# Replacing a list scheduler by written-out tables of order, engines, places and zero products in a two-layer transformer kernel

## The chip, the cores and the metric

The kernel runs on one core of one Trainium2 chip. The metric is the device time of one execution in microseconds (us). Engines are named as in the profile: PE is the matrix engine (TensorE), PEld its weight load, DVE is VectorE, ACT is ScalarE, POOL is GpSimd, and SP is SyncE, which here does nothing but issue DMAs. Each engine takes its instructions in the order in which the program lists them for it, and an instruction whose inputs are not ready holds up everything behind it on its engine.

## What is computed

The reference applies four residual blocks, each on a layer-normed input, to `x` of shape 8 x 512 x 128 in fp32:

```python
x = x + linear_attn(layernorm(x))     # 16 heads x 64; elu+1 features, q*KV/(q*Ksum+eps), wo, gelu
x = x + fp4_ffn(layernorm(x))         # both operands of each product rounded to blockwise FP4
x = x + causal_attn(layernorm(x))     # 16 heads x 8, softmax under a causal mask
x = x + routed_ffn(layernorm(x))      # rms norm, top 2 of 8 experts, low-rank (LoRA) experts on shared weights
```

The loop over the batch index b (0 to 7) is outermost; nothing of one b enters another b, so stages of different b can be run side by side.

## The kernel before, in words

`block_kernel` does not issue its instructions as it walks through the computation. Every call on `nc.tensor`, `nc.vector`, `nc.scalar`, `nc.gpsimd`, `nc.sync` or `nc.either` is recorded by `Plan.add` as a `Step`: one instruction, or several of one engine inside `one_go()`. There are 5166 steps. `nc.either` (the elementwise products of two SBUF tensors) leaves open whether DVE or POOL does the step. Only at the end does `plan.issue()` (line 1517) put all steps in an order, choose a buffer for each tile, and emit them; that is why nearly every row of the profile has one line, L407.

The stages are, for each b: `norm` (layer norm and transposition by `normed_T`, line 963), `linear` (`linear_attention`, line 978: for each of eight chunks of 128 features three 128x512 products on PE, elu on ACT and DVE, and for each pair of chunks in `products`, line 1015, one reciprocal of z0*z1 in two halves on DVE and five `either` products), `out` (`linear_out`, eight 128x512 products, gelu), `fp4` (`quantised`, line 1054: a chain of block maxima, scaling and rounding on DVE and `either`, followed by products), `attention` (`group`, line 1286: four groups of four heads; for each query tile the products of the next group's row maxima in `largest`, the products of this group in `scores`, the exponent on ACT, the causal cut on POOL, the product with v into `mid`), `routing`, and `experts` (line 1428: 34 products of 128x512 on PE for each b, a tanh on ACT, two multiply-adds on DVE and one `either` product for each of eight tiles). PSUM holds two tiles `pair` (two banks each), one `mid` and three `ahead`; an `ahead` tile can also be lent half a `pair`.

The order comes from `Plan.ordered` (line 249), a list scheduler: it walks along a planned time, and whenever an engine is free gives it the ready step of lowest rank. Ranks come from the table `TURNS` (line 706), which gives each stage of each b a span of due times. Durations come from the functions `cost` and `work`. The engines are asked in the order tensor, gpsimd, vector, scalar, sync, so that a ready `either` step is offered to POOL first. `Together` adds a dependence, that a group of products starts only when the inputs of all of them are ready. `Free` hands out the buffers. Last, `kept_warm` (line 365) puts products with zeros into planned gaps of PE (`plan.warmer`, line 907: a 128-row product of `ident` with zeros that is added to `mid`): they change no data and keep PE busy. 44 of them are issued, between 64 and 512 columns wide.

Of the kernel before, what the change touches and what calls it, by code (L numbers as in the profile page):

```python
# [17 lines left out]
P = 128  # L18
# [93 lines left out]
class Buf:  # L112


    def __init__(self, tag=None, place=None):
        self.tag, self.place = tag, place
        self.writer, self.readers = None, []
        self.first, self.users = None, {}


class Step:


    def __init__(self, number, engine, lane):
        self.number, self.engine, self.rank, self.lane = number, engine, 0.0, lane
        self.calls, self.needs, self.takes, self.uses = [], {}, [], {}
        self.cost, self.slow, self.port, self.size = 0.0, 0.0, False, 0
        self.work = 0.0
        self.start = self.end = None


TWO_PORTS = ("tensor_tensor", "scalar_tensor_tensor", "tensor_scalar", "tensor_copy")


class Plan:
# [3 lines left out]
    HOP = {"tensor": 0.1, "gpsimd": 0.1, "vector": 0.1, "scalar": 0.1, "sync": 0.2}  # L139

    def __init__(self, nc):
        self.nc, self.steps, self.open = nc, [], None
        self.lane, self.tags, self.psum, self.warmer = None, {}, (), None
        self.parts = {}
        self.engines = {n: Engine(self, n) for n in (*self.HOP, "either")}


    def tag(self, name, places, parts=None):

        self.tags[name] = list(places)  # L150
        self.parts[name] = parts or [((name, i),) for i in range(len(places))]
# [24 lines left out]

    def fixed(self, place):
        return View(Buf(place=place), place.shape)

# [4 lines left out]
    def together(self):  # L184
        return Together(self)

    def span(self, lane, low, high):
        return Span(self, lane, low, high)

    def add(self, engine, method, a, k):  # L190
        step = self.open
        if step is None:
            step = Step(len(self.steps), engine, self.lane)
            self.steps.append(step)
        elif step.engine is None:
            step.engine = engine
        assert step.engine == engine
        out = [k["out"]] if "out" in k else [a[0]]
        ins = [x for x in (*a[0 if "out" in k else 1 :], *k.values()) if isinstance(x, View)]
        if k.get("accum_out") is not None:  # L200
            out.append(k["accum_out"])
        step.calls.append((method, a, k))
        fast = "vector" if engine == "either" else engine
        if method is not None:
            step.cost += cost(fast, method, out[0], ins, a, k)
        if engine == "tensor" and method is not None:
            step.work += work(method, ins, a, k)
        if engine == "sync":
            step.size += 4 * out[0].shape[0] * _free(out[0])
        if engine == "either":  # L210
            step.slow += cost("gpsimd", method, out[0], ins, a, k)

        if engine == "gpsimd" and method != "memset":
            step.port = True
        elif engine in ("vector", "either") and method in TWO_PORTS:
            two = sum(v.shape[-1:] != (1,) or len(v.shape) > 2 for v in ins) > 1
            step.port |= (two or _free(out[0]) > 16) and not any(
                v.buf.tag in self.psum for v in (*ins, out[0]) if isinstance(v, View)
            )
        for v in ins:  # L220
            if all(v is not o for o in out) and isinstance(v, View):
                self.reads(step, v.buf)
        for v in out:
            if isinstance(v, View):
                self.writes(step, v.buf)

    def reads(self, step, buf):
        assert buf.writer is not None or buf.tag is None
        if buf.writer is not None and buf.writer is not step:
            step.needs[buf.writer] = True  # L230
        buf.readers.append(step)
        self.used(step, buf)

    def writes(self, step, buf):
        for s in (buf.writer, *buf.readers):
            if s is not None and s is not step:
                step.needs[s] = True
        buf.writer, buf.readers = step, []
        if buf.first is None and buf.tag is not None:
            buf.first = step  # L240
            step.takes.append(buf)
        self.used(step, buf)

    def used(self, step, buf):
        buf.users[step] = True
        step.uses[buf] = True


    def ordered(self):

        free = Free(self.parts)
        slots = {}
        left = {s: len(s.needs) for s in self.steps}
        then = {s: [] for s in self.steps}
        for s in self.steps:
            for n in s.needs:
                then[n].append(s)
        users = {}  # L260
        for s in self.steps:
            for b in s.uses:
                users[b] = len(b.users)
        ready_at = {s: 0.0 for s in self.steps}
        empties = set()
        for s in self.steps:
            for b in s.uses:
                if b.tag in self.psum and s.engine != "tensor" and (False or max(b.users, key=lambda u: u.number) is s):
                    empties.add(s)
        waiting = {e: [] for e in self.engines}  # L270
        for s in self.steps:
            if not left[s]:
                waiting[s.engine].append(s)
        turns = {}
        for s in sorted(self.steps, key=lambda s: (s.rank, s.number), reverse=True):
            for b in s.takes:
                turns.setdefault((s.lane, b.tag), []).append(b)
        busy = dict.fromkeys(self.engines, 0.0)
        port = 0.0
        moved = 0.0  # L280
        ends = []
        now, done, order, stuck = 0.0, 0, [], False
        clock = Clock()
        while done < len(self.steps):
            for e in self.HOP:
                while busy[e] <= now:
                    best, kept = None, set()
                    shared = waiting["either"] if e in ("vector", "gpsimd") else []
                    ready = [s for s in (*waiting[e], *shared) if ready_at[s] <= now]
                    ahead = HURRY if e == "tensor" and clock.idle(now) else 0.0  # L290
                    for s in sorted(
                        ready,
                        key=lambda s: (s.rank - (ahead if s.work > 0.6 * s.cost else 0.0) - (EMPTY if s in empties else 0.0), s.number),
                    ):
                        if s.port and port > now:
                            continue
                        asked = {}
                        for b in s.takes:
                            asked.setdefault(b.tag, []).append(b)
                        if not all(  # L300
                            all(b in turns[s.lane, t][-len(bs) :] for b in bs)
                            for t, bs in asked.items()
                        ):
                            continue
                        if all(
                            (t not in kept or stuck) and free.has(t, len(bs)) for t, bs in asked.items()
                        ):
                            best = s
                            break

                        kept.update(asked)
                    if best is None:
                        break
                    if any(
                        now < ready_at[s] <= now + PATIENCE and s.rank < min(best.rank - MARGIN, LIMIT)
                        for s in (*waiting[e], *shared)
                    ):
                        break
                    s, stuck = best, False
                    waiting[s.engine].remove(s)  # L320
                    if s.engine == "either":
                        s.engine = e
                        s.cost = s.slow if e == "gpsimd" else s.cost
                    for b in s.takes:
                        slots[b] = free.take(b.tag)
                        turns[s.lane, b.tag].remove(b)
# [6 lines left out]
                    if s.port:  # L333
                        port = busy[e]
# [1247 lines left out]
```

## Time and profile before

| | us |
|---|---|
| median of 3 runs | 1126.88 (1125.94 to 1127.14) |
| span of the profiled execution, first to last instruction | 1130.1 |
| PE busy in that span | 1040.2 (92%) |
| DVE busy | 830.3 (73%) |
| ACT busy | 630.8 (56%) |
| POOL busy | 624.3 (55%) |
| DMA engines, mean rate | 39 GB/s, of that 235 GB/s in the first 28 us |

No time but the span is given for the profiled execution itself; the span is 0.3% above the median of the three runs. In the profile's busy times the end of a product is modelled and lies behind the start of the next one, so that PE can be shown as fully busy while its products come at different distances. A product of fp32 operands stands as two rows in the profile. Of the DVE, successive instructions overlap by some 85 ns in the trace.

### The profile page before, as it was taken

The page shows a single profiled execution, that of the slowest core. Times are in us where ns is not written, and L with a number is a line of the kernel's source. Part 1 is how long each engine was busy: PE and PEld are TensorE (multiplying, and loading weights), DVE is VectorE, ACT ScalarE, POOL GpSimd, SP SyncE. Part 2 cuts the span into 40 slices and gives each one's busy share as a digit, 9 for nine tenths or more (in the row PEclk, how much of TensorE's full clock was granted, in tenths as well). Part 3 has the DMA queues.
Part 4 walks back from the last instruction along what each step waited for, and adds up shares of the span by engine and source line. Part 5 has one row for each costly group of instructions (what it writes and reads, how often), then busy time and mean ns, then how long its engine had stood idle before and what let it go on. Part 6 is the DMA issues. An engine that isn't in the chain of part 4 may idle for free.

```text
span 1130.1 us, 15043 instructions
## 1 busy us (share of the span) xinstructions
PE 1040.2 (92%) x5025; PEld 488.0 (43%) x5025; DVE 830.3 (73%) x1868; ACT 630.8 (56%) x1084; POOL 624.3 (55%) x669
## 2 busy tenths in 40 slices
PE   6667788998899999999998999999999999999998
PEld 2223333344344444444543444454454445445454
DVE  6868879897888967758788968788667765556543
ACT  5756787678786644644578555764443443344311
POOL 6647846676676466237635755467644533441534
PEclk9879989999999999999999999999999999999999
DMA  8000030001101020111012000210002102001000
GB/s 235 1 1 0 1 111 1 21 20 56 39 20 30 10 94 20 58 72 35 26 39 94 19 21 20 95 30 19 20 7 98 39 20 104 21 20 30 1 10 9
DMA packets 30572, 44.31 MB, mean 39 GB/s; under 512 B 4192, under 2 KB 18464, under 8 KB 30496
## 3 DMA queue, kind: packets, MB, share of 16 engines
q1 hardware_dynamic: 30496, 43.37, 11.9%
q8 instruction: 39, 0.64, 0.2%
q14 instruction: 37, 0.30, 0.1%
HBM read 23.95 MB, written 18.87 MB: 38 GB/s over the span
## 4 chain that ended last, share of the span: by engine, by line
PE 57%; DVE 15%; ACT 6%; issue 2%; POOL 1%; DMA 0%; POOLq 0%; DVEq 0%; ACTq 0%
PE ahead L407 31%; PE pair L407 19%; PE mid L407 7%; ACT pr L407 2%; DVE r L407 2%; DVE mx L407 2%; DVE h L407 1%; DVE sc L407 1%; ACT qf L407 1%; DVE s4 routing L407 1%; DVE qf L407 1%; DVE act L407 1%; ACT z L407 1%; DVE kf L407 1%; DVE oh L407 1%
## 5 line engine op out<-in xcount | busy, mean ns | idle before, releaser
L407 ACT ACTIVATE pr<-pair 128x1024 f32<-128x1024 f32 (+1 forms) x192 | 166.7, 879 | 149.2 <-PE pair L407 129.1
L407 DVE TENSOR_REDUCE mx<-pair 128x4 f32<-128x512 f32 (+2 forms) x192 | 198.5, 1041 | 68.4 <-PE pair L407 57.7
L407 POOL TENSOR_SCALAR_AFFINE_SELECT pr<-pr 128x256 f32<-128x256 f32 (+1 forms) x192 | 92.8, 485 | 176.4 <-ACT pr L407 175.6
L407 PE MATMUL pair<-qkT 32*128 32x128 f32 (+7 forms) x1024 | 172.3, 387 | 9.4 <-ACT pr L407 2.7
L407 PEld LDWEIGHTS pair<-qkT 32*128 32x128 f32 (+1 forms) x1024 | 84.4, 183 | 181.8 <-ACT pr L407 52.0
L407 POOL TENSOR_TENSOR act<-act,tw 128x512 f32<-128x512 f32 x64 | 81.3, 1272 | 88.8 <-DVE act L407 80.6
L407 PE MATMUL ahead<-um,b_sb 128*128 128x512 f32 x240 | 122.2, 607 | 0.0
L407 DVE RECIPROCAL r<-r 128x256 f32<-128x256 f32 x64 | 110.3, 1736 | 14.9 <-POOL r L407 14.8
L407 DVE SCALAR_TENSOR_TENSOR act<-act,ahead 128x512 f32<-128x512 f32 x120 | 81.9, 684 | 51.4 <-ACT act L407 38.0
L407 POOL TENSOR_TENSOR qa<-qa,qa 128x704 f32<-128x704 f32 (+4 forms) x60 | 81.2, 1354 | 35.1 <-DVE qa L407 26.2
L407 POOL TENSOR_TENSOR qf<-qf,r 128x512 f32<-128x512 f32 x64 | 80.5, 1278 | 34.5 <-DVE r L407 27.8
L407 PE MATMUL mid<-pr,va 128*10 128x512 f32 (+3 forms) x1024 | 93.3, 435 | 0.0
L407 POOL TENSOR_TENSOR qf<-qf,z 128x512 f32<-128x512 f32 x64 | 80.3, 1270 | 0.0
L407 ACT ACTIVATE act<-ahead 128x512 f32<-128x512 f32 x60 | 35.8, 597 | 72.0 <-PE ahead L407 71.9
L407 PE MATMUL ahead<-act,a_sb 128*128 128x512 f32 x128 | 65.2, 619 | 0.0
L407 POOL TENSOR_TENSOR r<-z,z 128x512 f32<-128x512 f32 x32 | 40.9, 1278 | 41.6 <-ACT z L407 39.3
L407 PE MATMUL ahead<-tT,w_sb 128*128 128x512 f32 x120 | 63.3, 609 | 0.0
L407 ACT ACTIVATE ahead<-ahead,bqkv_sb 128x512 f32<-128x512 f32 x96 | 63.0, 656 | 0.0
L407 PE MATMUL pair<-mask_q,ident 128*128 128x128 bf16 (+1 forms) x384 | 61.6, 242 | 0.0
L407 PE MATMUL ahead<-xnT,wk 128*128 128x512 f32 x100 | 56.7, 650 | 4.8 <-DVE kf L407 2.1
L407 PEld LDWEIGHTS ahead<-um,b_sb 128*128 128x128 f32 x240 | 40.7, 190 | 36.1 <-issue 29.6
L407 ACT ACTIVATE z<-qf,eps_sb,s 128x512 f32<-128x512 f32 x64 | 51.9, 811 | 6.8 <-DVE s L407 5.1
(227 smaller groups left out, 1986.4 us busy)
## 6 DMA issues: line engine op xcount, KB each, us to landing
stacks<-qk SPq DMA_DIRECT2D x32, 512.0 KB
qkT<-stacks SPq DMA_DIRECT2D x128, 128.0 KB
x<-in SPq DMA_DIRECT2D x8, 256.0 KB
qkT<-mr SPq DMA_DIRECT2D x128, 4.0 KB
out<-x SPq DMA_DIRECT2D x8, 256.0 KB
w_sb<-in SPq DMA_DIRECT2D x3, 256.0 KB
wq<-in SPq DMA_DIRECT2D x4, 128.0 KB
wk<-in SPq DMA_DIRECT2D x4, 128.0 KB
```

Of the source, the lines that this page charges most:

```text
L407: getattr(e, method)(*a, **k)
```

## The change

The scheduler goes: `Plan.ordered`, `kept_warm`, `Free`, `Together`, `Span`, `Clock`, `cost`, `work`, `TURNS` and every dependence that `Plan.add` kept for them. `Plan.issue` is given four tables instead: `ORDER`, the 5166 step numbers in the order in which they are issued; `ENGINES`, one letter for each `either` step; `PLACES`, one buffer number for each tile; and `ZEROS`, ten places in the order at which a product with zeros of a given width is put. Waits between engines are still set from the data that each instruction touches.

```diff
-    def issue(self):
-        for s in self.ordered():
-            for b in s.takes:
-                b.place = self.tags[b.tag][self.slots[b]]
+    def issue(self, order, engines, places, zeros):
+        engine = iter(engines)
+        for s in self.steps:
+            if s.engine == "either":
+                s.engine = {"v": "vector", "g": "gpsimd"}[next(engine)]
+        numbers = [
+            SIGNS.index(order[i]) * len(SIGNS) + SIGNS.index(order[i + 1])
+            for i in range(0, len(order), 2)
+        ]
+        assert sorted(numbers) == list(range(len(self.steps)))
+        place = iter(places)
+        for at, n in enumerate(numbers):
+            s = self.steps[n]
+            for b in s.takes:
+                b.place = self.tags[b.tag][int(next(place), 36)]
+            if at in zeros:
+                self.warmer(zeros[at])
             e = getattr(self.nc, s.engine)
...
+ORDER = (
+    "&3!!&1!H!K!I!)!J!L!O!N!M!P!Q!R!&!-$a$b!=!$$H$I$J!#$K$L$M!%$T$U$N!(!8&`&c$O!4$V$W!9!*$P!,"
...
+ENGINES = (
+    "vggggvggggvggggvgggggvvvgvggggggggvgggggvvggggvgggvggvggggggvggvgvgvgggggggggggggvvggggv"
...
+ZEROS = {
+    48: 512, 50: 384, 142: 512, 249: 256, 365: 192, 428: 512, 484: 512, 488: 320, 736: 512,
+    751: 256,
 }
...
     with tc.manual_schedule():
-        plan.issue()
+        plan.issue(ORDER, ENGINES, PLACES, ZEROS)
```

The recorded steps, their shapes and their number are the same in both kernels. Set side by side by engine, the two programs differ in this: 148 of the `either` steps that POOL does before are done by DVE after; 44 products with zeros become 10; and the order on every engine, SP's DMAs among them, is another.

## The prediction

> **What bounds the kernel now.** I first read the busy times of the page and then the same cut into four stretches. The cuts are not at equal times but at equal PE work. To get that work I took, for each kind of PE step, the start-to-start distance to the next step in the trace, and of each kind the lower quartile (the distance when nothing is late). These add up to 910 us for all steps but the products with zeros. The cuts stand where 150, 250 and 700 us of this work have been started.
>
> ```profile
> PE 1040.2 (92%) x5025; PEld 488.0 (43%) x5025; DVE 830.3 (73%) x1868; ACT 630.8 (56%) x1084; POOL 624.3 (55%) x669
> ```
> ```profile
> 0.00:247.20 247.20, 195.56 (x636) 84.08 (x637) 197.07 (x481) 170.82 (x300) 157.46 (x178) 0.93 0.15 45
> 247.20:372.80 125.60, 113.50 (x571) 52.99 (x570) 106.70 (x254) 95.97 (x174) 85.00 (x84) 1.00 0.10 35
> 372.80:884.70 511.90, 496.05 (x2614) 236.92 (x2613) 390.30 (x850) 280.55 (x477) 285.07 (x300) 1.00 0.13 43
> 884.70:1130.10 245.40, 235.14 (x1211) 113.99 (x1209) 136.25 (x285) 83.43 (x134) 96.74 (x108) 0.99 0.09 27
> ```
>
> The columns of the second view are the stretch, its length, busy PE, PEld, DVE, ACT, POOL, and PE's granted clock. A PE that is 92% busy looks as if nothing could be won. The timeline of PE in a dense place shows why that is misleading:
>
> ```profile
> 1091.71 1.02 PE L407 MATMUL ahead<-tT,w_sb 128*128 128x512 f32 x2
> 1092.57 1.02 PE L407 MATMUL ahead<-um,b_sb 128*128 128x512 f32 x2
> 1093.42 1.02 PE L407 MATMUL ahead<-tT,w_sb 128*128 128x512 f32 x2
> ```
>
> Each product is shown as 1.02 us long, but the next starts 0.86 us later. Counted so, the stretches lose 247 - 150 = 97 us, 126 - 100 = 26, 512 - 450 = 62 and 242 - 210 = 32 (its last product starts at 1126), 217 us together. Of this some 35 us have to be paid in any order: a 128-row product followed by one of the narrow attention products (32 rows, or 10 columns) starts the next one 95 ns later or more; there are 269 such changes before and 227 after, worth 26 and 22 us, and the head up to the first real product takes some 10.
>
> In the first stretch nothing is full: PE does 150 us of work in 247, and DVE, the busiest, stands at 80%. What it loses is waiting in a circle. The longest piece:
>
> ```profile
> 52.00:56.00 4.00, 0.00 (x0) 0.00 (x0) 3.30 (x13) 2.24 (x4) 2.51 (x3) 0.89 0.00 0
> 56.00:60.00 4.00, 0.00 (x0) 0.00 (x0) 2.73 (x2) 0.00 (x0) 3.68 (x3) 0.50 0.00 0
> ```
> ```profile
> 61.29 1.63 PE L407 MATMUL ahead<-ident,xn 128*128 128x128 f32 x4 [9.29 <-ACT xn L407]
> ```
>
> PE stands still for 9.3 us until the norm of b = 1 arrives, and the granted clock falls to 0.50.
>
> **The change, part by part.** *Engines.* 148 elementwise products go from POOL to DVE, 116 of 512 columns, 22 of 704 and 10 smaller.
>
> ```profile
> L407 POOL TENSOR_TENSOR act<-act,tw 128x512 f32<-128x512 f32 x64 | 81.3, 1272 | 88.8 <-DVE act L407 80.6 <-DVE s4 attention L407 5.2 <-DVE s4 routing L407 2.0
> L407 DVE SCALAR_TENSOR_TENSOR y<-y,y 128x512 f32<-128x512 f32 x8 | 5.9, 734 | 2.0 <-ACT y L407 2.0
> ```
>
> POOL takes 1.27 us for 512 columns. DVE does none of these before; the nearest row reads the same two SBUF tensors, has a median of 0.684 us, and occupies DVE for 0.60 (rows overlap by 0.085). So DVE gains 116 x 0.60 + 22 x 0.83 + 10 x 0.4 = 92 us (the wider ones scaled by width), and POOL loses 116 x 1.27 + 22 x 1.5 + 10 x 0.9 = 189. In total DVE goes to some 922 us, near PE's 910; POOL falls to 435. By itself each moved product makes its chain 0.59 us shorter, and costs every later DVE step up to 0.60 us. Bounds: if all are covered, nothing; if all stand in front of something that PE waits for, 92 us. I take nothing for the stretches in which DVE has room (below) and the whole in the first two, where it sets the length.
>
> *Zero products.* 34 fewer. They start some 0.84 us apart at full width, 40 us busy in all, but they stand in planned gaps; if the gap remains, nothing is won, and I count no gain. The danger is the clock. In the third stretch only five of the 44 stand before 850 us, two of them within 3 us of its start, and its clock is 1.00; the first stretch has most of them, and its clock is 0.93 all the same. So the clock follows PE's real work, and I count no loss. The Trainium skill speaks against the change here: "TensorE: Matmul & The Clock Gate", in "Part 1: The HAM clock gate", says that an idle window of about 3.4 us halves the clock. If each zero product removed let one such window go to half clock, that page would make it an estimated 34 x 3.4 / 2 = 58 us lost, and the sum below 1111 instead of 1053. The row of 56 to 60 us shows the halving; the third stretch shows that it does not need zero products to stay away.
>
> *Order.* This is the main part. For each PE step I followed its inputs back through the other engines to the last PE step on the way, summed the row durations of that round trip, and took off the PE work that stands between the two in PE's order. What is left is an index of the waits that the order has built in, not a time. For the first 150 us of PE work it is 63 us before and 25 after; from 150 to 250 it is 8 and 7; from 250 to 700, 19 and 21; beyond, 41 and 15. The same for DVE, over the first 150 us of PE work: 61 before, 4 after. The norm of b = 1 is one reason: its x is the 12th DMA on SP instead of the 24th, and its transposition stands within the first 20 us of PE work, not at 26.
>
> **The sum.** In stretch 1, DVE has 188 us of rows after (178 before). In its best piece before, PE work 120 to 150, DVE did 31.4 us in 34.9, 90%. With the built-in waits of DVE nearly gone I take 90% for all: 209 us, and 4 for the head: 213. Stretch 2: 107 us of DVE rows / 0.9 = 119. Stretch 3: PE 450, and of the 62 lost the change removes some 17: fewer changes of shape, and PE steps with a finished producer further ahead (beyond 200 us of PE work 71% of the steps that wait for another engine have its last step at least 1 us of PE work ahead, 56% before): 495. Stretch 4: 210, and of the 32 lost half remains, as the index falls from 41 to 15: 225. Sum 1052, and 4 us to the end of the output: a span of 1056 against 1130.1. The median of the runs lies 3 us under the span, so **1053 us**, 6.6% faster.
>
> SP's order is moved too. All weights come in the first 28 us at 235 GB/s, and some chunks (`wo` of chunk 0 from place 11 to 35) now land later, by up to 24 places x 0.128 MB / 235 GB/s = 13 us. I cost this at nothing: `out` of b = 0 has not started by then (47 us before). If that cover fails, it costs up to 13 us.
>
> **The rivals.**
>
> *Half the gain.* The orders of all engines are coupled: one late step on DVE moves all behind it. If stretch 1 runs at DVE's present 178 / 247 = 72%, the 188 us take 261, and only stretches 2 to 4 gain: 7 + 17 + 17 less 14 is 27, a time of 1100. Between this and the forecast, anything. For it: the moves make DVE the fullest engine where it is already fullest. Against it: the index of DVE's waits.
>
> *Slower: DVE sets the end.* Between 250 and 650 us of PE work 69 of the 148 products are added to DVE; they stand in front of the `mx` reductions and `act` multiply-adds that empty PSUM for PE. Price 0.60 us each, 92 us for all. It decides once more than 73 us of these 92, four in five, land on PE's path, or correspondingly fewer if the order gains less; with all of them and the forecast's gain it is 1053 + 92 = 1145. For it: PE's rows show waits for DVE `kf` of 17 us. Against: per 50 us of PE work in that part DVE has 40 to 53 us of rows, so only one such piece (600 to 650) is over PE's.
>
> *Nothing changes.* If the tables only wrote down what the scheduler had chosen, 1127. The orders side by side exclude the same order; an equal time would be chance.
>
> **How the numbers follow.** Forecast and its surroundings (1010 to 1085) 0.60; half the gain (1085 to 1124) 0.26; no difference 0.03; slower 0.11. A measurement of this kernel tells 0.2% from no change. Low end: stretch 1 at 194 + 4 and stretch 2 at 110 (DVE 97% full), 475 for stretch 3 and 220 for stretch 4 with the 4 of the end is 1007, a little under the range. The range of 1012 to 1112 leaves out about 2 in 10, most of it above. Faster 0.86, within 0.2% 0.03, slower 0.11.
>
> **What would show it.** The mark of 150 us of PE work near 213 instead of 247 us; no PE gap over 4 us after 15 us; the clock of the first stretch at 0.97 or more with ten zero products; DVE busy 920, POOL 435. I am wrong if the first stretch is no shorter, if PE's waits for DVE grow, or if the clock falls in later stretches.

## The result, and the profile after

The changed kernel takes 1178.01 us (median, 1169.85 to 1186.19), the kernel before on the same chip 1127.01: a ratio of 1.043, 95% interval 1.037 to 1.049. It is slower, and the forecast of 1053 us was wrong in size and in sign. The page of the profiled execution after, of 1176.7 us span: the busy times, the granted clock in 40 slices, and the shares of the chain that ended last.

```profile
PE 1047.8 (89%) x4957; PEld 493.8 (42%) x4957; DVE 919.1 (78%) x2016; ACT 633.2 (54%) x1084; POOL 451.7 (38%) x521
...
PEclk8998899999999989999999997988979999999999
...
PE 51%; DVE 35%; ACT 9%; issue 4%; POOL 2%; DVEq 0%; ACTq 0%; POOLq 0%
```

DVE's busy time is what the forecast said. The clock row has eights and sevens late in the run, where the page before has nines. In the chain DVE stands at 35%, before at 15%: PE waits for DVE more often than before. The same stretches as in the prediction, cut at equal PE work (columns as there):

```profile
0.00:238.40 238.40, 189.31 (x618) 79.60 (x618) 203.86 (x497) 168.93 (x298) 132.29 (x152) 0.94 0.15 46
238.40:362.10 123.70, 110.18 (x574) 52.33 (x574) 116.57 (x270) 95.37 (x168) 59.60 (x65) 1.00 0.11 35
362.10:931.50 569.40, 522.10 (x2545) 250.63 (x2543) 443.02 (x929) 283.87 (x481) 202.32 (x229) 0.93 0.11 38
931.50:1176.70 245.20, 226.22 (x1224) 111.23 (x1222) 155.69 (x323) 85.06 (x138) 57.53 (x76) 0.99 0.10 30
```

The first two stretches are 11 us shorter than before, the last is unchanged, and the third takes 569 us instead of 512 at a clock of 0.93 instead of 1.00. All of the loss arises there.

To see of what it consists, I took each product's distance to the next beyond the dense distance, and put it down to the half clock (up to a doubling), to a wait over 0.25 us, or to short gaps; from a product with zeros to the next product all is put down to the zeros. With some 910 us of dense work and 4 us up to the first product each row adds up to its last column. The sums, in us, of the kernels that matter below:

| | zeros | waits | half clock | short gaps | last product starts |
|---|---|---|---|---|---|
| before | 74 | 61 | 14 | 64 | 1126 |
| after | 20 | 139 | 50 | 50 | 1173 |
| after, more zeros (e1) | 95 | 86 | 14 | 49 | 1157 |
| after, other places (e11) | 19 | 93 | 30 | 51 | 1106 |
| e11, zeros in gaps (e14) | 57 | 58 | 6 | 51 | 1085 |

Zeros and waits belong together, since most zeros stand where PE would wait. From before to after that sum grows by 24 us, the half clock costs 36 more, and the short gaps 14 less, for fewer changes of shape.

**What PE waits for.** Of the waits of PE in the trace after, the three largest groups, and then a timeline of the end of one wait:

```profile
PE pair L212 <- DVE act L212: 18.7, 15, 2.3
PE pair L212 <- DVE mx L212: 9.7, 26, 0.9
PE pair L212 <- DVE kf L212: 9.3, 8, 3.1
```
```profile
795.17 0.68 DVE L212 SCALAR_TENSOR_TENSOR act<-act,pair 128x512 f32<-128x512 f32 x1
795.77 0.88 DVE L212 TENSOR_SCALAR qa<-qa 128x512 uint32<-128x512 uint32 x2
795.91 0.50 PEld L212 LDWEIGHTS pair<-xnT,wq 128*128 128x128 f32 x2 [2.52 <-DVE act L212]
795.91 2.08 PE L212 MATMUL pair<-xnT,wq 128*128 128x512 f32 x2 [2.26 <-DVE act L212]
```

The columns of the first view are what waits, for what, us in total, times, longest. Before, the first of these groups is almost nothing:

```profile
PE pair L407 <- DVE act L407: 0.5, 1, 0.5
```

The group of 18.7 us is odd: no product that waits here takes an input from `act`. In the timeline (start and length in us, engine, line, operation) a product of `linear` of b = 7 stands still for 2.26 us until a multiply-add of `experts` of another b has read its tile; both tiles stand as `pair`. By the kernel's tables the multiply-add reads the first half of a `pair` place and the product writes an `ahead` tile into the second half. They share no data and no bank, only the place.

For every wait of PE over 0.25 us I compared its end with the last end of all that the step needs: its inputs, and the readers of the last tile in its own half. Waits that last over 0.2 us longer than that are 41 with 47.6 us after, and 9 with 5.8 us before. All are steps on a lent half; 35 of the 41 end 49 to 64 ns after a DVE or ACT instruction that reads the other half. In the kernel before 119 PE steps on a lent half have a DVE or ACT instruction on the other half ahead of them in the order, after 350; not one of these steps starts before the last such instruction has ended. That waits are "set from the data that each instruction touches", as said above, is thus too narrow for these: they are set for the whole `pair` place. The Trainium skill, "PSUM — Partial Sum Buffer", in "PSUM bank collisions raise a hardware error", says that engines on different banks run without conflict; by that rule the chip does not need these waits. No run here does without the wait, so that is not shown.

### The profile page after: what moved, and what is told of

The parts are those of the page before. It is cut to its first block, busy times and chain, and to the rows that moved or that the text cites. A ratio compares the mean times of both kernels' runs of the same rounds, so it can differ in the third digit from the quotient of the medians.

```text
span 1176.7 us, 14801 instructions
## 1 busy us (share of the span) xinstructions
PE 1047.8 (89%) x4957; PEld 493.8 (42%) x4957; DVE 919.1 (78%) x2016; ACT 633.2 (54%) x1084; POOL 451.7 (38%) x521
## 4 chain that ended last, share of the span: by engine, by line
PE 51%; DVE 35%; ACT 9%; issue 4%; POOL 2%; DVEq 0%; ACTq 0%; POOLq 0%
PE pair L212 26%; PE ahead L212 20%; DVE mx L212 8%; DVE r L212 6%; PE mid L212 4%; DVE act L212 3%; DVE qf L212 3%; ACT pr L212 2%; DVE qa L212 2%; DVE kf L212 2%; DVE sc L212 1%; DVE h L212 1%; DVE ahead L212 1%; ACT qf L212 1%; ACT pair L212 1%
## 5 line engine op out<-in xcount | busy, mean ns | idle before, releaser
L212 DVE TENSOR_REDUCE mx<-pair 128x4 f32<-128x512 f32 (+3 forms) x192 | 198.2, 1040 | 57.2 <-PE pair L212 47.6
L212 PE MATMUL pair<-qkT 32*128 32x512 f32 (+7 forms) x1024 | 180.2, 401 | 20.7 <-DVE mx L212 9.5
L212 PE MATMUL ahead<-um,b_sb 128*128 128x512 f32 x172 | 91.1, 622 | 0.0
L212 POOL TENSOR_TENSOR act<-act,tw 128x512 f32<-128x512 f32 x32 | 42.2, 1324 | 104.7 <-DVE act L212 80.9
L212 POOL TENSOR_TENSOR qa<-qa,qa 128x704 f32<-128x704 f32 (+4 forms) x37 | 50.5, 1366 | 67.1 <-DVE qa L212 58.3
L212 PE MATMUL ahead<-qf,wk_o 128*128 128x512 f32 x104 | 56.0, 642 | 1.6 <-ACT wk_o L212 1.5
L212 PE MATMUL pair<-um,b_sb 128*128 128x512 f32 x84 | 44.3, 620 | 13.8 <-DVE act L212 8.5
L212 DVE SCALAR_TENSOR_TENSOR act<-act,pair 128x512 f32<-128x512 f32 x42 | 28.7, 684 | 30.9 <-ACT act L212 16.6
L212 ACT ACTIVATE qf<-qf,one_sb 128x512 f32<-128x512 f32 x64 | 45.9, 719 | 11.4 <-DVE qf L212 11.4
L212 PE MATMUL ahead<-xnT,wv 128*128 128x512 f32 x90 | 49.5, 637 | 2.5 <-DVE qf L212 1.9
```

Source lines behind the costliest of these rows:

```text
L212: getattr(e, method)(*a, **k)
```

## The experiments

The runs shared chips with runs of the kernel before, and each ratio is to those. "Half-clock us" is the time spent at half clock, not the time lost by it as in the table above. "Lent" is the number of `ahead` tiles (of 541) on a half of `pair`; "other half" the waits for the other half, as counted above. The replay is worked out from the rows: every engine takes its steps in order, each with the row's duration (PE's with the dense distance), 0.06 us from one engine to the next, no half clock and no zeros; once with each half waiting for itself, once with the whole place.

| run | us | ratio to before | half-clock us | lent | other half, us | replay: halves, whole |
|---|---|---|---|---|---|---|
| before | 1127.0 | 1 | 41 | 91 | 6 | 1053, 1068 |
| after | 1178.0 | 1.043 (1.037 to 1.049) | 113 | 225 | 48 | 1031, 1091 |
| e1_zeros | 1163.1 | 1.030 (1.027 to 1.033) | 31 | 225 | 40 | as after |
| e2_pool | 1177.8 | 1.043 (1.040 to 1.046) | 92 | 225 | 45 | 1043, 1103 |
| e3_engines | 1172.4 | 1.038 (1.035 to 1.041) | 58 | 91 | 7 | 1079, 1093 |
| e4_nozeros | 1143.1 | 1.012 (1.009 to 1.015) | 85 | 91 | 6 | as before |
| e5_own | 1211.1 | 1.070 (1.065 to 1.074) | 133 | 123 | 17 | 1092, 1116 |
| e6_lent | 1150.0 | 1.017 (1.013 to 1.020) | 58 | 212 | 19 | 1052, 1075 |
| e7_hybrid250 | 1140.3 | 1.008 (1.005 to 1.011) | 61 | 129 | 19 | 1042, 1073 |
| e8_hybrid150 | 1130.5 | 0.998 (0.996 to 1.000) | 44 | 114 | 17 | 1037, 1068 |
| e9_spread | 1208.7 | 1.068 (1.064 to 1.071) | 120 | 225 | 47 | 1054, 1111 |
| e10_more | 1129.5 | 0.998 (0.997 to 1.000) | 24 | 91 | 6 | as before |
| e11_places | 1111.1 | 0.980 (0.976 to 0.984) | 68 | 199 | 5 | 1031, 1036 |
| e12_before_places | 1116.2 | 0.986 (0.984 to 0.989) | 34 | 207 | 5 | 1048, 1048 |
| e13_hybrid_places | 1098.3 | 0.971 (0.968 to 0.974) | 17 | 197 | 3 | 1034, 1038 |
| e14_places_zeros | 1093.0 | 0.966 (0.963 to 0.970) | 14 | 199 | 4 | 1031, 1036 |
| e15_pool_too | 1116.2 | 0.987 (0.983 to 0.991) | 41 | 199 | 4 | 1045, 1050 |

**One part of the change at a time.** Four runs undo or do the parts that the tables hold.

*e1_zeros*: 62 more products with zeros in the changed kernel (20,544 columns; the number below is of all 72).
```diff
-    48: 512, 50: 384, 142: 512, 249: 256, 365: 192, 428: 512, 484: 512, 488: 320, 736: 512,
+    48: 512,
+    50: 384,
...
+    717: 512,
+    817: 512,
```


> The changed kernel's order, engines and places, with 62 more products with zeros (24,512 columns in all, about 41 us of PE) put where its profile shows PE's wide products below 60% of the last 3.4 us and PE waiting, or below 42% whether it waits or not. Theory C (the new order lets PE's clock fall: 112 us at half clock against 41 before, worth about 36 us between 250 and 700 us of PE work): half-clock time under 60 us, 1140 to 1165 us. Theory W (the waits come from the 148 products that DVE took over, and the clock only follows the waits): no faster than 1178, up to 1195, because the added products stand in front of real ones.

1163.1 us. In the third stretch the clock is back:
```profile
361.70:914.80 553.10, 515.19 (x2619) 250.85 (x2621) 442.00 (x929) 283.56 (x481) 203.04 (x229) 0.99 0.12 39
```
The half clock costs 36 us less, but zeros and waits together 22 us more, as some of the added products stand where there was no gap. The clock is part of the loss and not its whole.

*e2_pool*: the changed kernel with all 148 products back on POOL.
```diff
-    "vggggvggggvggggvgggggvvvgvggggggggvgggggvvggggvgggvggvggggggvggvgvgvgggggggggggggvvggggv"
+    "gggggggggggggggggggggggggggggggggggggggggggggggggggggggggggggggggggggggggggggggggggggggg"
```


> The changed kernel's order, places and zero products, with all 148 products back on POOL. Theory W: the extra waits of PE for DVE (about 42 us more than before in the waits over 0.25 us of the third stretch) go, 1130 to 1150. Theory C, or that the order itself is to blame: no gain, 1175 to 1210, as each product is 0.6 us longer on POOL and the order was written for DVE.

1177.8 us, the time of the changed kernel. Taking the products off DVE does not make it faster. As each takes 0.59 us longer on POOL, a gain and a loss can cancel here; e15 below shows that they do so only in this setting.

*e3_engines*: the reverse, the move to DVE alone in the order, places and zeros before.
```diff
-    "gggggggggggggggggggggggggggggggggggggggggggggggggggggggggggggggggggggggggggggggggggggggg"
+    "vggggvggggvggggvgggggvvvgvggggggggvgggggvvggggvgggvggvggggggvggvgvgvgggggggggggggvvggggv"
```


> The order, places and 44 zero products of the kernel before, written out as tables, with the changed kernel's engines: only the 148 products move to DVE. Theory W: 1150 to 1175, as DVE gets 92 us more work in front of evictions. Theory C: within 10 of 1127. As the prediction saw it, up to 10 faster where the first stretch is bound by POOL's chains.

1172.4 us, 3.8% above before. In an order that was not made for it, the move costs nearly half of the 92 us of DVE work, though DVE is busy for only 79% of the span.

*e4_nozeros*: the kernel before without any product with zeros.
```diff
+ZEROS = {
+}
```


> The order, places and engines of the kernel before, written out as tables, without any zero product (44 less). Theory C: more half-clock time, 60 to 90 us instead of 41, and 1140 to 1160 us. If zero products only fill gaps, as the prediction took it: within 5 of 1127.

1143.1 us, 1.2% above before, with half-clock time of 85 instead of 41 us. The loss of 34 of these 44 products I had counted at nothing; all 44 are worth 1.2%.

**Which tiles are lent.** Two runs change only `PLACES`, by the rule that a lent half is itself the cost.

*e5_own*: in the changed kernel `ahead` tiles go to the three places of their own where one is free in the order of the program, 123 instead of 225 on lent halves.
```diff
-    "00028630101130200061231045160a046003139112520111243212050104503606145001111a071284200206"
+    "00028630101130200012031045160a146000139212520111213012013104502606145001311a071084210202"
```


> The changed kernel with other PSUM places alone: of its 541 ahead tiles 123 instead of 225 lie in halves of the pair tiles, the rest in the three places of their own (316 tiles moved, the order, engines and zero products as they are). Theory P (lent halves leave attention one pair tile, so that its products wait for the exponent and the row maxima; such waits of PE for a pair place are 29 us between 250 and 700 us of PE work against 3 before): 1145 to 1165 us. Theory O (the order itself sets too little PE work between a step and what it waits for): within 8 of 1178.

1211.1 us, slower than the change itself: neither theory has it, and the cure that I had expected failed. Waits for the other half do fall, from 48 to 17 us, but places of their own are taken again sooner, and PE waits for their readers instead (the replay with halves apart rises from 1031 to 1092).

*e6_lent*: in the kernel before, 212 instead of 91 tiles are lent.
```diff
-    "0000012102010031112010001001231120000311324234140515261010723802144391a21020043b11043201"
+    "0000012102010031112013001004536120000111324234140535561610722802101394a21000345b11063202"
```


> The order, engines and zero products of the kernel before, with other PSUM places alone: 212 instead of 91 of the ahead tiles lie in halves of the pair tiles (the place that has been free longest is taken). Theory P: 1145 to 1165 us, with waits of PE for a pair place over 15 us. Theory O: within 6 of 1127.

1150.0 us, 1.7% above before. Lending costs something in that order too, with waits for the other half of 19 instead of 6 us. Together with e5, the number of lent tiles can't be the rule.

**Which part of the order.** Two kernels begin with the changed order and go on with the order before.

*e7_hybrid250* (cut at 250 us of PE work) and *e8_hybrid150* (at 150):
```diff
-    "2Y2ZC~2]2^2_2[313234>ED*D-2a-S2b2c2d2`2f2g2h33D!7bC}-P-Q-U-R2e2j2k7d7e>77f-V-W-Z-[-T>FD9"
+    "2Y2ZC~2]2^2_2[313234>ED*D-2a-S2b2c2d2`2f2g7b7d7e8;7f7g7h33357i>77j7k7lCs>F7m>G7n>H>I7oC|"
```
```diff
-    "6S6p0~6i*K*L*M+_+`+a+h+d6l7#7$+i7/7!70+f+g+k+e*N+l*O+o<`+p,,+m6q+w+x<a0W71+s+t73*R+y+z6r"
+    "6S6p0~6i*K*L*M+_+`+a+h+d6l7#7$+i7/7!70+f+g+k+e5u6>6q6]6d0W0X6r7D6t6s0Y7E0Z6u0[7F0]0^6v0_"
```


> The changed kernel's order, engines and places up to 250 us of PE work (1781 steps, 38 products on DVE), then the remaining steps in the order of the kernel before, on its engines, with its zero products. If the loss lies in the later order and its clock, and the first part is as good as its trace shows (250 us of PE work reached 11 us earlier): 1112 to 1122 us. If the changed kernel's start borrows from later stages: 1127 or more.

> The same cut at 150 us of PE work (1123 steps, 25 products on DVE), where the changed kernel is 9 us ahead. If the start is what is good in it: 1114 to 1124 us, and the second stretch on the order before adds its 126 us. If the start borrows: 1127 or more.

1140.3 and 1130.5 us, both as expected of a start that borrows. The third stretch takes 529 and 512 us with the tables before, 569 with the changed ones: most of the loss comes with the changed tables beyond 250 us of PE work. But after the longer start the third stretch is 17 us longer than before (512), so a part is owed to what the start leaves behind. Neither start brings more than 0.2%.

*e9_spread*: the changed kernel with 78 wide products moved into long runs of narrow attention products.
```diff
-    "=o1,={=|>!>#,t,u1X1Y>$1^1_1Z1[1]>)>*>+=r,v1b1m1-1c,y1`1a,x1n1d1.=p,w1g,z,{=q1e1f1h1i,}>,"
+    "=o1,={=|>!>#,t,u1X1Y>$1^1_>)1Z1[1]>*>+=r,v1b1-1m1c,y1`1a,x1n1d1.=p,w1/1g,z,{=q1e1f1h1i,}"
```


> The changed kernel with 78 wide products (128 rows by 512 columns) of PE moved earlier, 3.5 PE steps in the mean, into long runs of narrow attention products beyond 200 us of PE work; engines, places and zero products stay. Runs of narrow products longer than 2 us in the third stretch fall from 21 (53 us) to 14 (36 us). Theory 'runs' (the long runs of narrow products let the clock fall and leave the round trips behind them uncovered): half-clock time falls from 112 to some 70 to 85 us, waits of PE in the third stretch from 59 to some 45, and the time is 1150 to 1165. Rival 'places' (what counts is the order in which PSUM places come free, not what PE does meanwhile): within 8 us of 1178. Second rival: bringing wide products forward takes a place earlier than it comes free, and the time is over 1186.

1208.7 us: the theory of the runs fell, and the second rival came true. Half-clock time stays (120 us), waits grow (by some 23 us). What the runs of narrow products are worth by themselves can't be read from it.

*e10_more*: the kernel before with 13 more products with zeros.
```diff
+    149: 192, 169: 448, 359: 512, 649: 448, 707: 64, 849: 64, 893: 128, 2642: 192, 2872: 128,
+    2918: 64, 4743: 64, 4846: 256, 5015: 448,
```


> The kernel before, its order written out as tables, with 13 more products with zeros put into gaps that its trace shows where the granted clock is about to fall. If zero products still missing cost this order something, the time is 2 to 6 us below the kernel before (half-clock time 41 us falls to some 25). If it has as many as are worth anything, within 2 us; if their own time on PE outweighs it, 2 us above or more.

A ratio of 0.998, 2 us, on the border between the first two expectations: half-clock time falls to 24 us, and the time by next to nothing. The order before had about as many as are worth anything.

**The shared wait.** e9 left waits of PE to explain. Asking of each wait whether the last thing that the step needs had not been done long before gave the waits for the other half, and the replay with the whole place puts after (1091) behind before (1068), while the replay with halves puts it ahead (1031, 1053). So I let the replay with the whole place choose new buffer numbers for `pair` and `ahead`, by trying single changes and keeping those that shortened it, and changed nothing else.

*e11_places*: the changed kernel, other numbers for 334 tiles. *e12_before_places*: the kernel before, other numbers for 420 tiles.
```diff
-    "00028630101130200061231045160a046003139112520111243212050104503606145001111a071284200206"
+    "00028630101130202003121056160a042001139412520111203212010104506506145001311a071284210202"
```
```diff
-    "0000012102010031112010001001231120000311324234140515261010723802144391a21020043b11043201"
+    "0000012102014031513012001006034122000511324133140505161510722802144393a21010642b11053200"
```


> The changed kernel with other buffer numbers for 334 tiles of `pair` and `ahead` in PSUM; order, engines and the ten zero products stay, and 199 instead of 225 `ahead` tiles are lent half a `pair`. New theory 'shared wait': the waits between engines are set for the whole of a `pair` place, so that an `ahead` tile that is lent one half waits for the readers of the tile in the other half, which has nothing to do with it. In the trace 41 gaps of PE before a lent tile (48 us in all) end some 53 ns after such a reader, against 9 (6 us) before the change. A replay of the queues with the row durations gives the changed kernel 1091 us with such waits and 1031 without them, and the kernel before 1068 and 1053; the new numbers are chosen so that the replay with these waits falls to 1036. Expected by this theory: the waits of PE in the third stretch fall from 59 to 15 to 30 us, the half-clock time falls with them, and the time is 1100 to 1135. Rival 'round trips' (the order leaves PE too little between a product and the readers of its own tile, and the shared place does not matter): 1165 to 1190, as the number of lent tiles is nearly the same.

> The kernel before, its order written out as tables, with other buffer numbers for 420 tiles of `pair` and `ahead`, chosen in the same way; engines and the 44 zero products stay; 207 instead of 91 `ahead` tiles are lent half a `pair`. An earlier run that lent 212 tiles without regard to the other half took 17 us more than the kernel before. Theory 'shared wait': the replay falls from 1068 to 1048 us, and the time is 5 to 25 us below the kernel before, though as many halves are lent as in that run. Rival 'lending costs': 10 to 20 us above the kernel before, as in that run.

1111.1 and 1116.2 us. In the changed kernel the buffer numbers alone are worth 67 us, some 6%, and turn a loss of 4.3% into a gain of 2.0%, with nearly as many tiles lent (199, 225). The waits for the other half are 5 us instead of 48. By the first table zeros and waits together fall by 47 us and the half clock by 20, which is the whole of it. In the third stretch PE's waits fall from 59 to 36 us, less far than the 15 to 30 expected. The theory of the shared wait holds here, and the rival "round trips" falls. In the order before the same choice is worth 1.4%, with more than twice as many lent tiles as before and about as many as in e6, which lost 1.7%, so "lending costs" falls too.

But e12 is no second proof of the shared wait. Its waits for the other half are 5 us and were 6 before; its gain lies in PE's other time (zeros and waits together fall from 135 to some 123 us, the half clock from 14 to 12). The replay had put it down to the shared place (1068 to 1048, with halves 1053 to 1048). So how buffer numbers act where little is lent is not shown.

The page and stretches of e11:

```profile
PE 1021.2 (92%) x4957; PEld 488.8 (44%) x4957; DVE 916.8 (83%) x2016; ACT 632.4 (57%) x1084; POOL 451.5 (41%) x521
...
PEclk9999999998999988999999998989999979999999
```
```profile
0.00:215.00 215.00, 175.29 (x618) 75.54 (x618) 203.37 (x497) 168.69 (x298) 132.42 (x152) 1.00 0.17 51
215.00:340.40 125.40, 114.64 (x575) 54.67 (x575) 116.77 (x270) 95.34 (x168) 59.64 (x65) 0.96 0.10 35
340.40:869.20 528.80, 500.46 (x2549) 245.29 (x2551) 441.54 (x929) 283.43 (x481) 202.06 (x229) 0.96 0.12 41
869.20:1110.20 241.00, 230.82 (x1224) 113.26 (x1222) 155.08 (x322) 84.98 (x138) 57.42 (x76) 0.96 0.10 31
```

Same instructions on the same engines in the same order, and the first stretch falls from 238 to 215 us, the third from 569 to 529. PE's mean clock rises with it (0.95 to 0.97), though it has the same ten zeros; in the second and the last stretch it falls, to 0.96. In the view of waits the group `PE pair <- DVE act` falls from 18.7 us to 1.9. The first is now one that has a reason, a tile's own reader, and it is as long as in the changed kernel:

```profile
PE pair L212 <- DVE mx L212: 9.7, 24, 1.1
PE pair L212 <- DVE kf L212: 5.7, 4, 2.4
...
PE pair L212 <- DVE act L212: 1.9, 3, 0.9
```

**What is left.** *e14_places_zeros*: e11 with 34 more products with zeros, only in gaps of its trace. *e13_hybrid_places*: e8's order with numbers chosen in the same way. *e15_pool_too*: e14 with the 148 products back on POOL (the edit of e2).
```diff
+    210: 64,
+    223: 192,
+    300: 256,
...
```
```diff
-    "00028630101130200061231045160a046003139112520111243212050104503606145001111a071284200206"
+    "00028630101130202004211065160a140002139412520111213212036104505106145001611a071284200203"
```


> The changed kernel with the new buffer numbers of the run before and 34 more products with zeros, 6848 columns in all, only in gaps of PE that this run's trace shows. There the granted clock is still half for 68 us, which is 30 us of lost time by the decomposition. Theory 'clock as a term of its own': half-clock time falls to some 30 us, the time by 8 to 18 us to 1093 to 1103. Rival 'the clock is only a consequence of the waits': within 4 us of 1111, as the gaps are filled either way.

> The start of the changed order up to 150 us of PE work, the order, engines and zero products before beyond that, and new buffer numbers for `pair` and `ahead` chosen by the replay with shared waits. With the old numbers this order took 1130.5 us. Theory 'shared wait': the replay falls from 1068 to 1038 us, and the time to 1095 to 1110, below the run with the changed order and new numbers (1111) since the rest has its zero products. Rival (the start's gain is lost again later whatever the places): 1115 or more.

> The version with the new buffer numbers and 34 more zero products (1093 us), with all 148 moved products back on POOL; nothing else changes. With the buffer numbers of the change the same edit made no difference (1178 us both times). If the waits for the other half had only hidden what the move is worth, the time is 6 to 16 us above 1093 (the replay says 1036 and 1050 us). If the move is worth nothing in this order, within 4 us. If the load on DVE is a burden, as it was in the order before (42 us), below 1089.

e14 takes 1093.0 us, 18 below e11 (1.4% by the ratios) and 3.4% below before, the fastest of all. Its clock and third stretch:

```profile
PEclk9999999999999999999999999999999999999999
```
```profile
338.40:854.20 515.80, 492.73 (x2573) 243.14 (x2571) 441.03 (x929) 283.07 (x481) 202.28 (x229) 1.00 0.13 42
```

Zeros and waits together stay (112 us in e11, 115 in e14), and the half clock falls from 30 to 6: the clock is a term of its own, and zeros in gaps cost nothing here. e13 takes 1098.3 us. So the changed order beyond 150 us of PE work, with its engines and with zeros put into its gaps, is worth some 5 us (0.5%), in place of the loss that it showed; even so its third stretch is the longer one (516 us, 508 in e13). e15 takes 1116.2 us: without the shared waits the move to DVE is worth 23 us, more than the 6 to 16 expected, where with them it was worth nothing. The buffer numbers and zeros of e14 were chosen with the products on DVE, so part of the 23 may be theirs.

## Why the prediction was wrong, point by point

**The step that failed is the order's index of built-in waits** ("For each PE step I followed its inputs back ... 63 us before and 25 after; ... 19 and 21"). It followed inputs and the last tile in the same buffer, and took the halves of `pair` as buffers of their own. Counted with the whole place it is 75, 12, 21, 41 before and 36, 10, 31, 24 after: the third stretch, which I had as unchanged, gets half as much again, with 134 more lent tiles. In its place the runs show 48 us of waits for the other half, against 6 before, and 67 us that other buffer numbers alone bring back (e11). Mending the index would not have been enough: its sum still falls, from 149 to 101. Only the replay, which has the queues of all engines, gives the sign (1068 before, 1091 after).

That the order was read rightly for the first stretch, e11 shows: with the waits gone, the mark at 150 us of PE work stands at 215 us, where the forecast had 213. In the change it stands at 238. With shared waits and half clock both nearly gone (e14), the span is 1089.5 us against 1056 in the forecast; of the 33 us left, 6 stand in the first two stretches, 21 in the third and 6 in the last.

**Zero products: wrong.** "So the clock follows PE's real work, and I count no loss." The evidence was that the third stretch ran at 1.00 with five zeros; it did not show that it would with other waits. It fell to 0.93, and the half clock costs 36 us more than before. Adding zeros brings back 15 us in the changed order (e1) and 18 in e11 (e14), and the 44 of the order before are worth some 14 (1.2% of 1127, e4). The skill's rule, which I had weighed and put aside, had the sign right; the estimate of 58 us from it was three to four times too large for what more zeros bring back.

**Engines: the sizes right, the price wrong.** DVE has 919 us (922 forecast); POOL 452 instead of 435, in part since its remaining 512-column products take 1.31 us on the mean in place of 1.27. To count nothing where DVE has room was no rule: the move costs 42 us by e3, nothing by e2, and brings 23 by e15. What a moved product costs is decided by the order around it and not by DVE's share of busy time. That DVE at 90% would set the first two stretches fits e11 (DVE busy for 203 us of 215 and 117 of 125; before, 197 of 247 and 107 of 126).

**Third stretch.** Of the 17 us that fewer changes of shape and a longer lead were to bring, the short gaps gave 10.5 (35.3 to 24.8). The lead of 71% instead of 56% showed no gain even in e14, whose third stretch takes 516 us against 495 forecast and 512 before. PE's waits over 0.25 us are some 26 us there, 17 before. Why is left open.

**SP's order** cost nothing that can be seen: e11's first stretch, with the same DMAs, comes out 2 us from the forecast.

**From span to time.** The last term of the sum, 3 us off, had the wrong sign: the execution profiled after took 1178.8 us at a span of 1176.7.

**Rivals.** Slower had 0.11, by "DVE sets the end". Slower is what came, by another mechanism: e2 and e11, with the same 148 products off and on DVE, exclude that one. Of the signs that I had named for being wrong, two appeared: PE's waits for DVE grew, and the clock fell in a later stretch. The clock of the first stretch, forecast at 0.97 or more, was 0.94. No PE gap after 15 us exceeds 4 us, as said, and that was no sign of anything.

## What to carry to other kernels

Before counting on a new order or new buffers, ask for each wait not only when its inputs are done but what else shares the buffer that the wait is set for; parts of a tile lent to other tiles can wait for each other without sharing data. In a trace, look for waits whose named releaser gives the waiting instruction nothing. A gain in order and a loss in buffers can hide each other, and so can the worth of any third edit: the same move to DVE was +42, 0 and -23 us in three surroundings, the last of them made for it.

## What the runs showed of the hardware

The granted clock is 1.0 or 0.5 and changes only at multiples of 3.41 us from one fixed time of each run: the 16 half-clock stretches of the changed kernel, without one that its end cuts off, are 3.4 to 20.5 us long. PE need not be idle for it. The 3.41 us before one fall of the clock, two stretches at half clock, all of the changed kernel, and one product in the first of these two:

```profile
961.15:964.56 3.41, 3.28 (x25) 1.98 (x28) 1.67 (x6) 2.73 (x5) 1.15 (x3) 1.00 0.00 0
718.00:736.00 18.00, 17.42 (x80) 8.73 (x79) 9.30 (x11) 9.56 (x17) 7.09 (x10) 0.53 0.00 0
848.00:869.00 21.00, 21.00 (x79) 9.07 (x78) 14.79 (x30) 10.15 (x18) 6.48 (x9) 0.51 0.05 14
```
```profile
720.14 2.08 PE L212 MATMUL ahead<-xnT,wk 128*128 128x512 f32 x2
722.01 0.63 PE L212 MATMUL ahead<-w_sb,act 128*128 128x128 f32 x2
```

PE is shown busy for 96% of the first row, which ends with the fall. In the 3.41 us before the 16 falls the share lies between 16% and 96%. In the other two PE is busy for 97% and 100%, at a clock of 0.53 and 0.51, and the 128x512 product takes 1.87 us to the next instead of 0.86. These two are full of narrow attention products of 32 or 34 rows. The Trainium skill, "TensorE: Matmul & The Clock Gate", "Part 1: The HAM clock gate", has the two states and the window of 3.4 us as seen here, but speaks of idle windows; these rows are not idle. What counts as activity is not settled: e9, which broke up the narrow runs, did not shorten the half-clock time, though its waits grew too, while 34 products with zeros in gaps took it from 68 to 14 us.
